# Low-rank adapters of the first token block: by batch in four column quarters, with x at the head of the load queue

## The chip, the cores and the metric

The kernel runs on one core of a Trainium2 chip. Its metric is the device time of one execution in microseconds (us). The engines named here are TensorE (PE; its weight loads are listed apart as PEld), VectorE (DVE), ScalarE (ACT), GpSimd (POOL) and SyncE (SP), which computes nothing and issues most transfers. A queue is the list of transfers that one engine issues, in order.

## The reference

Eight batches of 256 tokens with 1024 features each are the input x. Every batch names one of eight low-rank adapters; its output feeds a gated feed-forward network with FP8 weights and activations, and x is added at the end:

```python
Bx  = einsum('bnr,...->bnr', x, B[adapter_ids])     # rank 16
c   = einsum('bnr,bor->bno', Bx, A[adapter_ids])    # 1024 features
xq  = fp8(clip(c / in_scale))                       # 1024 -> 2752 gate and up
hid = silu(xq @ gate.T * s) * (xq @ up.T * s)
out = x + fp8(hid / in_scale) @ down.T * s          # 2752 -> 1024
```

## The kernel before

Everything is transposed: features lie on the 128 partitions, tokens in the free dimension. The 2048 tokens are four blocks (`NTB`) of 512 (`TB`), two batches of 256 (`SEQ`) in each. The 1024 features are 8 rows (`NH`) of 128, numbered k. The 2752 hidden features are 22 chunks (`NI`), the last one half full.

The program builds its instructions in one pass; an engine takes its own in the order in which they are written, and `multiply` and the copies around it are held to that order. What starts when is then decided by the waits.

**The loads at the start** (lines 394 to 421 of the kernel before). SP issues: the first half of block 0's x (k 0 to 3, 1 MB); a value load of the adapter id of batch 1 and that batch's B (`load_b`, line 366; 68 KB, with the scales of the network in its last columns); x of k 4 to 6; four pieces of A (`load_a_two`, line 373; 16 rows of 2 KB each, two for each batch); x of k 7; the gate and up weights of chunk 0 in two halves and of chunks 1 to 4 whole, 1 MB each (`load_gate_up`, line 391); then block 1's and the other blocks' B, x and A. ScalarE's queue carries the ids and the B of batch 0. GpSimd's queue carries no transfer. A load can start only when the one eight places before it, on the same completion counter, has landed.

**The adapters of a block of two batches** (`two_times_b` and `two_times_a`). TensorE works here with four groups of 32 columns or rows at a time. In B, the four groups are the two batches and two halves of each batch's 256 tokens, so a matmul has 128 columns; for each k four matmuls go to the four groups, into two result tiles `bx`. The 32 stationary columns of a group are 16 of the batch's B and 16 beside them, and A has zeros in the rows of those. Two copies on VectorE and two on ScalarE bring the results into a tile `bm` in which every group's half is beside the other half, so that A can work with all four groups: each row group holds a half of A's output features for one batch. A makes tiles `c` of 2 k rows, VectorE and ScalarE scale them and round them to FP8 (`round_to`, lines 526 and 528) into `xg[t]`.

For block 0 TensorE first does 16 matmuls of zeros (`pass_time`), then B of k 0 to 3, four more matmuls of zeros, B of k 4 to 7, seven of zeros while the copies run, and A.

**Chunk 0** of block 0 is `gate_up(0, 0, turns=(2, 2, 2, 2))`: 16 matmuls of 512 columns, gate and up in turns of two k, so that it can begin when the first rounded rows are there. Chunks 1 to 4 of block 0 follow, then the adapters of block 1 (inside chunk 4), and so on. Blocks 2 and 3 share a pass of four batches (`four_times_b`).

**The output.** For each k of the 8 output rows `times_down` adds up the 22 chunks and `finish` (line 695) multiplies by the scale and adds x. The last k takes its x from a second load into the space of `xg[0]` and `xg[1]`, since it runs in another branch of the program (line 753).

Of the kernel before, what the change touches and what calls it, by code (L numbers as in the profile page):

```python
# [9 lines left out]
F32 = mybir.dt.float32  # L10
# [25 lines left out]

KS = NH // 2

PIECES = ((4, 3, 1), (4, 3, 1), (NH,), (NH,))
FP8_MAX = 448.0  # L40

SAME_MAX = 240.0
# [14 lines left out]
    return ap.bitcast(U16)[..., 0::2]  # L57


def x_of(x4, t, k):  # L60

    first = 0
    for n in PIECES[t]:
        if k < first + n:
            break
        first += n
    at = (t * NH + first) * P * TB
    piece = x4[at : at + n * P * TB].rearrange("(p k n) -> p k n", p=P, k=n)
    return piece, first


def x_row(x4, t, k):
    piece, first = x_of(x4, t, k)
    return piece[:, k - first, :]


def gate_up_of(w_gu, c):
# [15 lines left out]
def general(  # L93
# [71 lines left out]
    def adapt(t, lora, b_sb, a_sb):  # L165
        bx = psum.tile([P, TB], F32, tag="ps", name="g_bx")
        for k in range(NH):
            xk = lora.tile([P, TB], F32, tag="xk", name="g_xk", bufs=2)
            nc.sync.dma_start(out=xk, in_=x_row(x4, t, k))
            nc.tensor.matmul(  # L170
                bx, lhsT=b_sb[:, k, :], rhs=xk, start=(k == 0), stop=(k == NH - 1)
            )
        bm = lora.tile([P, TB], F32, tag="bm", name="g_bm")
        for j in range(TB // SEQ):
            b = t * (TB // SEQ) + j
            nc.vector.tensor_scalar(
                bm[:, bass.ts(j, SEQ)],
                bx[:, bass.ts(j, SEQ)],
                mask[:, b : b + 1],
                None,  # L180
                ALU.mult,
            )
        for k in range(NH):
            c = psum.tile([P, TB], F32, tag="ps", name="g_c")
            nc.tensor.matmul(
                c, lhsT=a_sb[:, bass.ts(k, P)], rhs=bm, start=True, stop=True
            )
            for to, s in ((xg, GATE_IN), (xu, UP_IN)):
                v = work.tile([P, TB], F32, tag="v", name="g_v")
                nc.scalar.activation(v, c, AF.Copy, scale=inv[:, s : s + 1])  # L190
                quantize(to[:, k, :], v, P)
# [38 lines left out]
    def down(t, hid):  # L230
        for k in range(NH):
# [25 lines left out]
                    stop=(i == len(tail) - 1),  # L257
                )
            xr = work.tile([P, TB], F32, tag="g", name="g_xr")
            nc.sync.dma_start(out=xr, in_=x_row(x4, t, k))  # L260
            o = work.tile([P, TB], F32, tag="v", name="g_o")
            nc.vector.scalar_tensor_tensor(
                o, in0=y, scalar=down_s, in1=xr, op0=ALU.mult, op1=ALU.add
# [20 lines left out]
def adaln_ffn(  # L284
# [52 lines left out]
    with ExitStack() as fast:  # L337
# [2 lines left out]
        work = fast.enter_context(tc.tile_pool(name="work", bufs=3))  # L340


        xs = [acts.tile([P, NH, TB], F32, name=f"x{t}") for t in range(NTB)]
        xg += [acts.tile([P, NH, TB], FP8, name=f"xg{t}") for t in range(2, NTB)]


# [2 lines left out]

        b_two = [lora.tile([P, 2 * BROW + R], F32, name=f"b{t}") for t in range(2)]
        a_two = [lora.tile([P, H // 2], F32, name=f"a{t}") for t in range(2)]

        b_four = lora.tile([P, 4 * BROW + R], F32, name="b_four")
        a_four = lora.tile([P, H], F32, name="a_four")
        nc.gpsimd.memset(a_two[0], 0.0)
        nc.vector.memset(a_two[1], 0.0)
        for b, n in ((b_two[0], 2), (b_two[1], 2), (b_four, 4)):
            nc.vector.memset(b[:, n * BROW :], 0.0)  # L360

# [5 lines left out]
                out=b[:, i * BROW : (i + 1) * BROW], in_=b8[bass.ds(adapter * P, P), :]  # L367
            )

        def load_a_two(t, j, adapter):  # L370
            for g in range(2):
                row = 32 * (2 * g + j) + R * j
                nc.sync.dma_start(
                    out=a_two[t][row : row + R],
                    in_=a8[bass.ds(adapter * 2 * R + g * R, R), :],
                )

        def load_x(t, k):
            piece, first = x_of(x4, t, k)
            ks = slice(first, first + piece.shape[1])  # L380
            nc.sync.dma_start(out=xs[t][:, ks, :], in_=piece)

        w_of = {}

# [6 lines left out]
                nc.sync.dma_start(out=w[:, bass.ts(i, n)], in_=src[:, bass.ts(i, n)])  # L391
            w_of[c] = w

        load_x(0, 0)
        load_b(b_two[0], 0, adapter_of(0, nc.scalar), nc.scalar)
        second = adapter_of(1, nc.sync)
        load_b(b_two[0], 1, second, nc.sync)


        load_x(0, 4)  # L400
        load_a_two(0, 1, second)
        load_a_two(0, 0, adapter_of(0, nc.sync))
        load_x(0, 7)
        for c in range(NFIRST):
            load_gate_up(c, parts=1 if c else 2)
        adapters = [adapter_of(2 + q, nc.sync) for q in range(6)]
        for j in range(2):
            load_b(b_two[1], j, adapters[j], nc.sync)
        for k in (0, 4, 7):
            load_x(1, k)  # L410
        for j in range(2):
            load_a_two(1, j, adapters.pop(0))

        for t in (2, 3):
            load_x(t, 0)
# [64 lines left out]
                    stop=(i == n - 1),  # L480
                )

        def times_b(bx, b, n, quads, between=None):


            for k in range(NH):
                for q, (i, row, t, cols) in enumerate(quads):
                    at = i * BROW + k * R - row
                    multiply(
                        bx[q][32 * q : 32 * (q + 1)],  # L490
                        lhsT=b[:, at : at + 32],
                        rhs=xs[t][:, k, cols],
                        start=(k == 0),
                        stop=(k == NH - 1),
                    )
                if between:
                    between(k)

        def two_times_b(t, between=None):


            n = SEQ // 2
            quads = [
                (j, R * j, t, slice(at, at + n))
                for half in range(2)
                for j in range(2)
                for at in (j * SEQ + half * n,)
            ]
            bx = [psum.tile([P, n], F32, tag="ps", name=f"bx{half}") for half in range(2)]
            times_b([bx[q // 2] for q in range(4)], b_two[t], n, quads, between)  # L510
            bm = lora.tile([P, 2, n], F32, tag="bm2", name="bm2", bufs=2)
            for other in range(2):
                for half, copy in enumerate((nc.vector.tensor_copy, nc.scalar.copy)):
                    to = half ^ other
                    tc.keep_in_program_order(
                        copy(  # L516
                            bm[64 * to : 64 * (to + 1), other],
                            bx[half][64 * half : 64 * (half + 1)],
                        )
                    )  # L520
            return bm

        def round_to(to, c, engine):
# [3 lines left out]
            else:  # L527
                nc.scalar.activation(to, c, AF.Copy, scale=scale, saturate=False)  # L528

        def two_times_a(t, bm):  # L530


            n = SEQ // 2
            for part in range(2):
                cs = [psum.tile([P, 2, SEQ], F32, tag="ps", name=f"c{q}") for q in range(4)]
                for other, i in product(range(2), range(2)):
                    for q in range(4):
                        rows = slice(32 * q, 32 * (q + 1))
                        multiply(
                            cs[q][:, i, bass.ts(q // 2 ^ other, n)],  # L540
                            lhsT=a_two[t][rows, bass.ts(2 * part + i, P)],
                            rhs=bm[rows, other],
                            start=True,
                            stop=True,
                        )
                for q in range(4):
                    k = KS * part + 2 * (q // 2)
                    to = xg[t][:, k : k + 2, bass.ts(q % 2, SEQ)]
                    round_to(to, cs[q], nc.vector if q % 2 else nc.scalar)

        def four_times_b():
            quads = [(q, 0, 2 + q // 2, bass.ts(q % 2, SEQ)) for q in range(4)]
            bx = psum.tile([P, SEQ], F32, tag="ps", name="bx")
            times_b([bx] * 4, b_four, SEQ, quads)
            bm = lora.tile([P, SEQ], F32, tag="bm", name="bm", bufs=2)
# [76 lines left out]

        warm = psum.tile([P, TB], F32, tag="ps", name="warm")
        pass_time(warm, 16, TB)
        bm = two_times_b(0, lambda k: pass_time(warm, 4) if k == 3 else None)
        pass_time(warm, 7)
        two_times_a(0, bm)
        gate_up(0, 0, turns=(2, 2, 2, 2))
        for c in range(1, NFIRST - 1):
            gate_up(c, 0)  # L640
# [49 lines left out]

        def finish(k, t, cols, y, x):
            o = outs.tile([P, TB], F32, tag="o", name="o")[:, cols]
            at = slice(t * TB + cols.start, t * TB + cols.stop)
            tc.keep_in_program_order(
                nc.vector.scalar_tensor_tensor(  # L695
                    o, in0=y, scalar=down_s, in1=x, op0=ALU.mult, op1=ALU.add
                )
            )
            tc.keep_in_program_order(nc.sync.dma_start(out=outT[bass.ts(k, P), at], in_=o))
# [30 lines left out]
        for k in range(NH - 1):  # L730
# [9 lines left out]
            if last:  # L740
                ws_last = load_down(k + 1)
                x_last = []

                blocks = x4.rearrange("(t n) -> t n", t=NTB)
                srcs = (
                    blocks[:2, bass.ts(k + 1, P * TB)].rearrange("t (p n) -> p t n", p=P),
                    blocks[2:].rearrange("t (p k n) -> p t k n", p=P, n=TB)[:, :, k + 1, :],
                )
                for i in range(2):
                    x = xg[i].rearrange("p k n -> p (k n)").bitcast(F32)  # L750
                    x = x.rearrange("p (t n) -> p t n", n=TB)
                    x_last += [x[:, j, :] for j in range(2)]
                    nc.sync.dma_start(out=x, in_=srcs[i])
            first = k % 2 == 0
            if first:
                tiles = down_tiles(NTB)
# [128 lines left out]
```

## Time and profile before

| what | us |
|---|---|
| median of 3 runs | 476.14 |
| lowest, highest | 475.85, 476.36 |
| the profiled execution, its own time | 477.12 |
| its span | 475.3 |
| PE busy | 469.8 |
| DVE busy | 105.6 |
| ACT busy | 192.5 |
| POOL busy | 1.0 |

The span runs from the first to the last instruction of the profiled execution; 1.8 us of its time lie around it. Busy time of an engine is the union of its instructions' spans; matmuls overlap, so a busy PE is not one at its peak. In a row of the timeline stand the start and the length in us, the engine, the source line, the operation and its tiles, the number of instructions merged, and in brackets how long the engine had been idle and who released it. In the windows, a transfer share of 1.00 means that all 16 transfer engines were busy.

### The profile page before, as it was taken

What the parts mean: (1) busy time and instruction counts of PE and PEld (TensorE: products, weight loads), DVE (VectorE), ACT (ScalarE), POOL (GpSimd) and SP (SyncE); (2) the same over time, 40 slices, a digit from 0 to 9 for tenths busy, and PEclk for the clock granted to TensorE, in tenths of its full rate; (3) what the DMA queues carried; (4) which work ended last, traced back from release to release, by engine and by line L of the source; (5) the groups of instructions that cost most, each with busy time, mean ns of one, the idle gap of its engine ahead of it and who ended that gap; (6) DMA issues with size and microseconds to landing.
All of it is one profiled execution on the core that took longest, in us unless ns stands there. A gap on an engine that the chain in (4) does not pass through costs nothing.

```text
span 475.3 us, 6009 instructions
## 1 busy us (share of the span) xinstructions
PE 469.8 (99%) x2514; PEld 217.0 (46%) x2514; DVE 105.6 (22%) x163; ACT 192.5 (40%) x249; POOL 1.0 (0%) x7
## 2 busy tenths in 40 slices
PE   8999999999999999999999999999999999999997
PEld 4454544444444444444444444444444444444444
DVE  1333432121212222121212212132120121031031
ACT  1322447995556654533454554359212022021000
POOL 0000000000000000000000000000000000000000
PEclk9999999999999999999999999999999999999999
DMA  8995013422222112222211111123335255063031
GB/s 291 406 405 186 1 48 133 176 88 90 88 88 89 24 66 89 90 88 88 90 30 60 44 62 56 61 83 123 103 146 161 64 185 161 22 213 114 3 116 66
DMA packets 13780, 53.44 MB, mean 112 GB/s; under 512 B 1650, under 2 KB 2930, under 8 KB 10674
## 3 DMA queue, kind: packets, MB, share of 16 engines
q1 hardware_dynamic: 13600, 52.92, 32.1%
q8 instruction: 21, 0.34, 0.3%
q14 instruction: 13, 0.11, 0.1%
q10 hardware_dynamic: 146, 0.07, 0.0%
HBM read 44.60 MB, written 8.39 MB: 111 GB/s over the span
## 4 chain that ended last, share of the span: by engine, by line
PE 96%; DMA 3%; SPq 0%; issue 0%; DVE 0%
PE y L470 62%; PE yd L470 31%; DMA w_gu<-w_gu 2%; PE c L470 1%; PE bx L470 1%; DMA x<-x 1%; DMA ids_i<-ids 0%; SPq L363 0%; SPq L366 0%; DVE o L695 0%; PE count L470 0%
## 5 line engine op out<-in xcount | busy, mean ns | idle before, releaser
L470 PE MATMUL y<-xg,w_gu 128*128 128x512 fp8e4 x1376 | 298.4, 379 | 0.9 <-DMA w_gu<-w_gu 0.9
L470 PEld LDWEIGHTS <-w_gu 128*128 128x128 bf16 x1376 | 134.0, 98 | 163.8 <-DMA w_gu<-w_gu 1.8
L470 PE MATMUL yd<-hid,w_d 128*128 128x512 fp8e4 (+2 forms) x693 | 146.0, 373 | 0.0
L609 ACT ACTIVATE g<-y,gate_s 128x512 f32<-128x512 f32 (+1 forms) x88 | 59.8, 681 | 137.2 <-PE y L470 137.2
L610 DVE SCALAR_TENSOR_TENSOR hid<-y,up_by_down,g 128x512 fp8e4<-128x512 f32 x84 | 63.1, 751 | 220.3 <-PE y L470 162.2
L470 PEld LDWEIGHTS <-w_d 128*128 128x128 bf16 x693 | 66.6, 98 | 79.0 <-issue 1.7
L456 ACT ACTIVATE junk<-w_d 128x1408 bf16<-128x1408 uint16 (+1 forms) x16 | 21.2, 1324 | 88.4 <-DMA w_d<-w_d 88.3
L695 DVE SCALAR_TENSOR_TENSOR o<-yd,down_s,x 128x512 f32<-128x512 f32 x28 | 20.0, 748 | 107.4 <-PE yd L470 92.8
L456 ACT ACTIVATE junk<-w_gu 128x2048 bf16<-128x2048 uint16 (+1 forms) x22 | 41.0, 1863 | 0.0
L463 ACT ACTIVATE junk<-hid 128x2048 bf16<-128x2048 fp8e4 x21 | 40.0, 1905 | 0.4
L463 ACT ACTIVATE junk<-xg 128x2048 bf16<-128x2048 fp8e4 x8 | 15.3, 1909 | 0.3
L528 ACT ACTIVATE xg<-c,inv 128x512 fp8e4<-128x512 f32 x16 | 9.7, 688 | 8.6 <-PE c L470 8.6
L526 DVE TENSOR_SCALAR xg<-c,inv 128x512 fp8e4<-128x512 f32 x16 | 10.9, 744 | 2.8 <-PE c L470 2.8
L470 PE MATMUL warm<-zeros 128*128 128x512 bf16 (+1 forms) x27 | 6.5, 402 | 1.2 <-DVE zeros L309 1.2
L695 DVE SCALAR_TENSOR_TENSOR o<-yd,down_s,xg 128x512 f32<-128x512 f32 (+2 forms) x5 | 3.2, 644 | 12.3 <-PE yd L470 12.3
L516 ACT COPY bm<-bx 64x128 f32<-64x128 f32 x4 | 1.0, 262 | 9.7 <-PE bx L470 9.6
L470 PE MATMUL bx<-x,b 128*32 128x128 f32 x128 | 4.3, 276 | 0.6 <-DMA x<-x 0.6
L470 PEld LDWEIGHTS <-zeros 128*128 128x128 bf16 x27 | 2.6, 116 | 4.7 <-issue 3.0
L470 PE MATMUL c<-bm,a 32*128 32x128 f32 x128 | 4.3, 277 | 0.0
L456 ACT ACTIVATION_READ_ACCUMULATOR junk<-w_gu 128x1 f32 x22 | 4.2, 191 | 0.0
L470 PEld LDWEIGHTS c<-bm,a 32*128 32x128 f32 x128 | 3.9, 186 | 0.5 <-ACT bm L516 0.4
L470 PE MATMUL yd<-hid_tail,w_dt 64*128 64x512 bf16 (+1 forms) x32 | 4.1, 377 | 0.0
(47 smaller groups left out, 41.0 us busy)
## 6 DMA issues: line engine op xcount, KB each, us to landing
w_gu<-w_gu SPq DMA_DIRECT2D x20, 1024.0 KB, 4.8
outT<-o SPq DMA_DIRECT2D x31, 256.0 KB, 2.2
w_d<-w_d SPq DMA_DIRECT2D x8, 704.0 KB, 4.8
w_d<-w_d SPq DMA_DIRECT2D x8, 640.0 KB, 3.9
x<-x SPq DMA_DIRECT2D x2, 2048.0 KB, 11.1
x<-x SPq DMA_DIRECT2D x2, 1024.0 KB, 8.6
x<-x SPq DMA_DIRECT2D x2, 768.0 KB, 9.5
w_gu<-w_gu SPq DMA_DIRECT2D x3, 512.0 KB, 3.8
```

Of the source, the lines that this page charges most:

```text
L456: nc.scalar.activation(junk_like(w), low(w), AF.Copy, accum_out=lows[:rows, column : column + 1])
L463: nc.scalar.activation(junk_like(q), q, AF.Square, accum_out=squares[:rows, column : column + 1])
L470: tc.keep_in_program_order(nc.tensor.matmul(*args, **kwargs))
L516: copy(bm[64 * to : 64 * (to + 1), other], bx[half][64 * half : 64 * (half + 1)],)
L526: nc.vector.tensor_scalar(to, c, scale, None, ALU.mult, saturate=False)
L528: nc.scalar.activation(to, c, AF.Copy, scale=scale, saturate=False)
L609: nc.scalar.activation(g[rows], gates, AF.Silu, scale=gate_s[: gates.shape[0]])
L610: nc.vector.scalar_tensor_tensor(to, in0=ups, scalar=up_by_down[rows], in1=g[rows], op0=ALU.mult, op1=ALU.mult, saturate=False,)
L695: nc.vector.scalar_tensor_tensor(o, in0=y, scalar=down_s, in1=x, op0=ALU.mult, op1=ALU.add)
```

## The change

Block 0's adapters are done batch by batch. `one_times_b(j)` gives each of the four groups a quarter of one batch's 256 tokens, so a matmul has 64 columns, and its stationary columns are that batch's for all four. `one_times_a(j, bm)` has the two quarters beside each other and makes 128 columns a matmul. Each row group needs its own 16 rows of A, so a batch's A is loaded four times (two halves of A, each twice), into a tile of its own. The order on TensorE becomes: 16 matmuls of zeros, B of batch 0, seven of zeros, A of batch 0, B of batch 1, seven of zeros, A of batch 1, chunk 0. The roundings are 256 columns instead of 512, and twice as many. Block 1 keeps its pass.

In memory, block 0's x is laid out by batch, and in pieces: batch 0 with k 0 to 3 and k 4 to 7, batch 1 with k 0 to 6 and k 7. SP issues these four first and the weights of chunks 0 to 4 right behind them. ScalarE's queue loads both batches' B, each after a value load of its id; GpSimd's queue loads both batches' A, each batch's four pieces after a value load. What comes after the weights on SP is as before. The second load of x for the last k becomes five loads instead of two, and `finish` reads block 0's x as two runs of 256.

```diff
-PIECES = ((4, 3, 1), (4, 3, 1), (NH,), (NH,))
+PIECES = (
+    ((0, SEQ, 0, 4), (0, SEQ, 4, 4), (SEQ, SEQ, 0, 7), (SEQ, SEQ, 7, 1)),
+    ((0, TB, 0, 4), (0, TB, 4, 3), (0, TB, 7, 1)),
+    ((0, TB, 0, NH),),
+    ((0, TB, 0, NH),),
+)
...
-        xs = [acts.tile([P, NH, TB], F32, name=f"x{t}") for t in range(NTB)]
+        x_first = acts.tile([P, 2, NH, SEQ], F32, name="x0")
+        xs = [x_first.rearrange("p j k n -> p k j n")]
+        xs += [acts.tile([P, NH, TB], F32, name=f"x{t}") for t in range(1, NTB)]
...
-        a_two = [lora.tile([P, H // 2], F32, name=f"a{t}") for t in range(2)]
+        a_one = [lora.tile([P, H // 2], F32, name=f"a0{j}") for j in range(2)]
+        a_two = lora.tile([P, H // 2], F32, name="a1")
...
-        load_x(0, 0)
-        load_b(b_two[0], 0, adapter_of(0, nc.scalar), nc.scalar)
-        second = adapter_of(1, nc.sync)
-        load_b(b_two[0], 1, second, nc.sync)
-        load_x(0, 4)
-        load_a_two(0, 1, second)
-        load_a_two(0, 0, adapter_of(0, nc.sync))
-        load_x(0, 7)
+        for i in range(len(PIECES[0])):
+            load_x(0, i)
+        for j in range(2):
+            load_b(b_two[0], j, adapter_of(j, nc.scalar), nc.scalar)
+            adapter = adapter_of(j, nc.gpsimd)
+            for q in range(4):
+                load_a_half(a_one[j], q, q // 2, j, adapter, nc.gpsimd)
         for c in range(NFIRST):
             load_gate_up(c, parts=1 if c else 2)
...
+        def one_times_b(j):
+            n = SEQ // 4
+            x = x_first[:, j]
+            quads = [
+                (j, R * j, x[:, :, at : at + n])
+                for half in range(2)
+                for at in (half * n, (2 + half) * n)
+            ]
+            bx = [psum.tile([P, n], F32, tag="ps", name=f"bx{half}") for half in range(2)]
+            times_b([bx[q // 2] for q in range(4)], b_two[0], n, quads)
+            bm = lora.tile([P, 2, n], F32, tag="bm1", name="bm1", bufs=2)
+            for other in range(2):
+                for half, copy in enumerate((nc.vector.tensor_copy, nc.scalar.copy)):
+                    to = half ^ other
+                    tc.keep_in_program_order(
+                        copy(
+                            bm[64 * to : 64 * (to + 1), half],
+                            bx[half][64 * half : 64 * (half + 1)],
+                        )
+                    )
+            return bm
...
+        def one_times_a(j, bm):
+            n = SEQ // 2
+            for part in range(2):
+                cs = [psum.tile([P, 2, n], F32, tag="ps", name=f"c{q}") for q in range(4)]
+                for i, q in product(range(2), range(4)):
+                    rows = slice(32 * q, 32 * (q + 1))
+                    multiply(
+                        cs[q][:, i],
+                        lhsT=a_one[j][rows, bass.ts(2 * part + i, P)],
+                        rhs=bm[rows].rearrange("p a n -> p (a n)"),
+                        start=True,
+                        stop=True,
+                    )
+                for g, half in product(range(2), range(2)):
+                    k = KS * part + 2 * g
+                    at = j * SEQ + half * n
+                    round_to(
+                        xg[0][:, k : k + 2, at : at + n],
+                        cs[2 * g + half],
+                        nc.vector if half else nc.scalar,
+                    )
...
         pass_time(warm, 16, TB)
-        bm = two_times_b(0, lambda k: pass_time(warm, 4) if k == 3 else None)
-        pass_time(warm, 7)
-        two_times_a(0, bm)
+        for j in range(2):
+            bm = one_times_b(j)
+            pass_time(psum.tile([P, TB], F32, tag="ps", name="warm"), 7)
+            one_times_a(j, bm)
         gate_up(0, 0, turns=(2, 2, 2, 2))
...
-                    nc.sync.dma_start(out=x, in_=srcs[i])
+                    for t in (2 * i, 2 * i + 1):
+                        for at, src in x_rows(x4, t, k + 1):
+                            nc.sync.dma_start(out=x_last[t][:, at], in_=src)
```

## The prediction

> **What bounds the kernel now.** I read the page's totals and its chain of waits first, then the chain in order of time, then the timeline of the first 17 us, then the same stretch cut into windows.
>
> ```profile
> span 475.3 us, 6009 instructions
> PE   469.8 (99%) x2514; PEld 217.0 (46%) x2514; DVE 105.6 (22%) x163; ACT 192.5 (40%) x249; POOL 1.0 (0%) x7
> PE y L470 62%; PE yd L470 31%; DMA w_gu<-w_gu 2%; PE c L470 1%; PE bx L470 1%; DMA x<-x 1%; DMA ids_i<-ids 0%; SPq L363 0%; SPq L366 0%; DVE o L695 0%; PE count L470 0%
> ```
>
> TensorE is the bound, so only its idle time and the start of its steady work can move. The chain in order of time (start, length, what) says where that start is:
>
> ```profile
> 3.33 4.97 DMA x<-x
> 8.30 0.02 issue
> 8.32 8.85 DMA w_gu<-w_gu
> 17.17 0.05 issue
> 17.21 13.12 PE y L470 x60
> 30.34 1.88 PE bx L470 x64
> ...
> 58.69 264.29 PE y L470 x1224
> 322.98 121.08 PE yd L470 x570
> ```
>
> From 17.21 us TensorE works without a stop to 472.5; 60 matmuls in 13.12 us are 0.219 each. Before it the chain is transfers: the second weight tile (chunk 1) lands at 17.17. A change to the first 17 us moves the end one for one, by what it does to the start of chunk 1 (call it S, now 17.2). The timeline there:
>
> ```profile
> 6.71 1.08 PE L470 MATMUL bx<-x,b 128*32 128x128 f32 x32
> 9.59 0.43 PE L470 MATMUL bx<-x,b 128*32 128x128 f32 x8 [0.38 <-DMA x<-x]
> 10.05 0.60 DVE L516 COPY bm<-bx 64x128 f32<-64x128 f32 x2 [3.46 <-PE bx L470]
> 10.45 2.17 PE L470 MATMUL c<-bm,a 32*128 32x128 f32 x64
> 11.68 2.73 DVE L526 TENSOR_SCALAR xg<-c,inv 128x512 fp8e4<-128x512 f32 x4 [1.03 <-PE c L470]
> 12.58 1.89 PE L470 MATMUL y<-xg,w_gu 128*128 128x512 fp8e4 x8
> 14.70 1.90 PE L470 MATMUL y<-xg,w_gu 128*128 128x512 fp8e4 x8 [0.23 <-DMA w_gu<-w_gu]
> ```
>
> The adapters finish at 12.58, chunk 0 needs 16 x 0.219 = 3.5 us and could end at 16.1; it waits for the second half of its weights and then chunk 1 waits to 17.2. So the adapters have about 1.1 us to spare, and the transfers have none. How full the transfers are (length, busy of PE, PEld, DVE, ACT, POOL, clock, DMA share, GB/s):
>
> ```profile
> 3.00:7.50 4.50, 4.50 (x42) 2.06 (x43) 0.51 (x6) 0.00 (x0) 0.00 (x0) 1.00 1.01 406
> 7.50:8.50 1.00, 0.78 (x24) 0.41 (x20) 0.00 (x0) 0.00 (x0) 0.00 (x0) 1.00 0.70 168
> 11.50:17.20 5.70, 4.86 (x55) 2.34 (x49) 3.00 (x5) 3.11 (x5) 0.00 (x0) 1.00 0.99 387
> ```
>
> They are full but for one hole, 7.5 to 8.5 us, where the four A loads pass and the last x and the weights were issued late (6.62 and 7.09 us).
>
> **What the Trainium skill says.** DMA: Bandwidth & Descriptors, section on issuing engines, says that DMAs of all issuers share the 16 engines and a second issuer saves issue time only. The trace agrees: the b issued by ScalarE landed 3.2 us after its issue, that by SP 3.3. Its sections Specifications and Anatomy of one DMA price a GpSimd (software) DMA at about 1 us to the first byte and 2.0 us + bytes/436 GB/s in all; no GpSimd DMA is in this trace. TensorE: Matmul & The Clock Gate, section "Wait — 56ns, not 53.3ns?", gives a floor of about 25 ns between starts of small matmuls; the trace's nearest row is 30 ns (64 records in 1.88 us at 128 columns). The same page, section "What's actually happening", says that an idle window of about 3.4 us halves the clock; the trace, whose longest gap is under 1 us, shows 1.0 throughout.
>
> **The change part by part.**
>
> *Issue order.* SP now issues four x pieces and the weights from 0.75 us on, some 0.42 us each, with no value load, b or A in between; the first weights go out at about 2.4 us, not 7.09. Since the engines are full from 3.0 us, this only closes the hole. Idle engine time there is about 5 us of 16 engines (from the packet records, 11 of 16 busy for 1 us), so it gives back 0.3 us of every later landing. SP then reaches its six value loads some 4.7 us earlier, and what follows (b, x and A of block 1) is bound by bandwidth anyway: it lands up to 31 us in a stream that stays full to 41.
>
> *More bytes.* A of block 0 goes from four 32 KB loads to eight, a quarter for each row group. A packet of 2 KB took 84 ns by the packet records, plus 59 in the mean for contention (16 rows lie on few ports): 4 more x 0.143 = 0.57 us on every engine. Smaller x rows (4 KB took 159 ns against 154 for half of an 8 KB one; 1 KB rows) add about 0.1. Sum: -0.3 + 0.57 + 0.1 = +0.36. Chunk 1 then lands at 17.17 + 0.36 = 17.5. Ends: the landing records show that 11 of the 16 engines had their part of chunk 1 by 15.0, and the slowest lags 2.4 us behind the median 14.8. Without that lag it is 15.1; with a further 1 us of it from the new queue, 18.5. I take 17.5, because nothing in the edit touches what the lagging engines did between 10 and 14.6 us.
>
> *Adapters on TensorE.* Before: one pass over both batches, split by k as x lands. After: batch 0 whole, batch 1 whole. The first matmul still starts at 6.71, behind the 16 passes of zeros. One B of a batch has 64 records of 64 columns: 64 x 25 ns = 1.6 us by the skill's floor (0.95 if half of the 1.88 row, 1.88 if columns save nothing). Four copies 0.55 (10.05 to 10.65 above; shorter tiles may save 0.1): A starts at 8.86. A of a batch is half of the 2.17 row, 1.08: to 9.95. Batch 1 takes over the first result buffers, so it waits for their rounding: 8.86 + 0.54 + 0.12 + 0.49 = 10.0. The 0.49 is a 128x256 rounding on VectorE, between the 0.351 (128 columns) and 0.750 (512) of the final multiply-adds; 0.12 is the hand-over seen from 11.52 to 11.64. B of batch 1 ends at 11.6 (its x lands near 9.3, not binding), copies 12.15, half of A 12.7, first rounding 13.3. So chunk 0 starts at 13.3, 0.7 later than now, and ends at 16.8. Ends: with the low B price 15.5, with the high one 17.4. The other roundings, eight per engine where there were four, come at 0.49 for each 0.87 of matmuls: hidden.
>
> *GpSimd's queue.* It holds 1.0 us of work before; now two value loads and eight A loads, one after the other. The first can go at about 2.9 (ScalarE's first after the same wait went at 2.88), the second value load takes about 0.6. With d per load, and 2.08 - 1.0 = 1.1 from its end to landing (the skill's prices), the last A lands at 2.9 + 0.6 + 8d + 1.1 = 4.6 + 8d, and S from it is 0.54 + 0.12 + 0.49 + 3.5 = 4.65 later: 9.25 + 8d. I take d = 1.0 (the first-byte price): A at 12.6, S = 17.25, just under the 17.5. Ends: d = 0.42 (SP's row with its registers) gives 12.6, hidden; d = 2.08, nothing overlapped, gives 25.9. What waits behind a late A is all of TensorE's stream.
>
> *ScalarE's queue.* Two b loads, at 2.9 and some 0.9 later; the second lands near 7.3 and is needed by the last k of batch 0, at about 8.1. Hidden with 0.8 to spare.
>
> *The end.* Five loads for the last x instead of two: three more at 0.4 us on SP, which after 317.83 + 2.10 waits till 323.04 for TensorE: hidden. The final multiply-add reads block 0's x in two runs; VectorE is idle 107 us before that group: hidden.
>
> *Sum.* S = max(16.8, 17.5, 17.25) = 17.5, against 17.2: +0.3 us. The profiled execution would go from 477.12 to 477.4 (span 475.3 to 475.6, 1.8 around it). The median of the runs is 476.14, 1.0 below the profiled one; the same step gives 476.5.
>
> **The rivals.**
>
> *A comes late.* The one mechanism that ends on the slow side: the second batch's A in GpSimd's queue. It decides from d = 1.03 us, and passes 0.2% (0.95 us, about what a measurement of this kernel can tell from no change) at d = 1.11. At d = 1.3 S is 19.65: +2.5 us, 478.6. For it: eight loads in series, each through software. Against it: 16 rows a load are few descriptors. If TensorE then also idles past a clock window, about 3.4 us run at half speed, 1.7 us more: near 480.3.
>
> *The lag goes and the small matmuls are cheap.* Chunk 1 lands at 15.1, and TensorE, at 0.95 us a B, is ready at 15.5: S = 15.5, -1.7 us, 474.4. For it: most engines deliver by 15. Against it: it needs both, and d under 0.78.
>
> *The lag goes alone.* TensorE bounds at 16.8: -0.4 us, 475.7, which is inside the likeliest case's range.
>
> **How the numbers follow.** Start bound by transfers or by TensorE within 0.2% of now: 0.50 (476.5, own range 475.6 to 477.1). A late: 0.36 (477.1 to 479.4), A late with the clock down: 0.06. Start clearly earlier: 0.08. So faster 0.08, same 0.50, slower 0.42. The range leaves out most of the early case and the far end of the late one: 475.3 to 479.4.
>
> **What would show it.** Right: chunk 1's first matmul waits for w_gu at about 17.5; no hole of transfers at 7.5 to 8.5; chunk 0 starts near 13.3; each B pass of a batch takes 1.6 us. Wrong: a wait of c for A's load with TensorE idle before the second batch's c (GpSimd late); chunk 1 running straight on from chunk 0 (the lag gone); a clock below 1.0 in the first slices; or TensorE waiting at block 1's bx near 30 us, which I cost at nothing.

## The result, and the profile after

| | before | after |
|---|---|---|
| median | 476.25 | 484.24 |
| lowest, highest | 475.85, 477.19 | 483.03, 484.74 |
| the profiled execution | 477.12 | 484.74 |
| its span | 475.3 | 483.1 |
| TensorE's first matmul of block 1's adapters | 30.34 | 38.02 |

The changed kernel takes 1.0161 of the time before (95% interval 1.0137 to 1.0185), 8.0 us more, where the prediction had 476.5 and at most 479.4. The last row is the shortest way to the place: of the span's 7.8 us, 7.7 are there before block 1 begins, and from there to the end both kernels take 445 us. So all of it arises in the first 25 us, where the prediction looked for the effect, but it is 7.7 us where 0.3 was forecast.

The page's span, clock row and chain of waits of the changed kernel:

```profile
span 483.1 us, 6191 instructions
...
PEclk8899999999999999999999999999999999999999
...
PE y L484 62%; PE yd L484 31%; PE c L484 2%; DMA b<-b 2%; PE bx L484 1%; PE warm L484 0%; ACT L313 0%; ACTq L375 0%; ACTq L378 0%; ACTq L312 0%; ACT xg L564 0%; DVE o L759 0%; PE count L484 0%
```

The weights and x, which stood in the chain before, are gone from it; B has come in. The two 8s in the clock row are new as well: in the first 24 us TensorE lost full speed twice. The chain in order of time (start, length, what) shows the new path:

```profile
4.16 7.46 DMA b<-b
...
11.65 0.44 PE bx L484 x8
...
17.20 2.13 issue
...
19.82 18.20 PE y L484 x76
38.02 1.89 PE bx L484 x64
```

Three things are to be seen. The load of batch 1's B, issued by ScalarE at 4.16, takes 7.46 us to land, and the last eight matmuls of batch 0's B wait for it, since the 32 stationary columns of its last k reach into the columns of batch 1. Then a gap of 2.13 us stands inside A of batch 1 with nothing that the profile can name ("issue"). And 76 matmuls of `y` take 18.20 us, where 16.5 is their time at full clock (0.216 to 0.219 us each in the steady stretches of both kernels). TensorE's own timeline (start, length, engine, line, operation, in brackets idle time and releaser):

```profile
9.87 2.22 PE L484 MATMUL bx<-x,b 128*32 128x64 f32 x64 [2.55 <-DMA b<-b]
...
14.20 1.14 PE L484 MATMUL bx<-x,b 128*32 128x64 f32 x64
...
19.33 0.49 PE L484 MATMUL c<-bm,a 32*128 32x128 f32 x3 [2.13 <-issue]
```

The first B matmul starts at 9.87, not 6.71: its B landed at 9.74, 6.7 us after its issue. Before, the same instruction on the same queue took 3.2. And the windows of this stretch (length, busy of PE, PEld, DVE, ACT, POOL, clock, share of the transfer engines, GB/s):

```profile
7.50:8.50 1.00, 0.00 (x0) 0.00 (x0) 0.00 (x0) 0.00 (x0) 0.80 (x2) 1.00 1.02 352
8.50:11.50 3.00, 1.63 (x56) 1.51 (x56) 0.51 (x6) 0.00 (x0) 0.48 (x1) 0.68 1.03 310
11.50:15.00 3.50, 3.33 (x105) 2.68 (x105) 1.72 (x6) 1.75 (x6) 0.00 (x0) 0.79 1.05 301
15.00:17.20 2.20, 2.17 (x60) 1.71 (x50) 1.14 (x4) 1.07 (x5) 0.00 (x0) 1.00 1.03 417
...
19.80:23.30 3.50, 3.50 (x10) 1.28 (x10) 0.48 (x1) 0.41 (x1) 0.00 (x0) 0.51 1.02 414
```

The hole of the transfers at 7.5 to 8.5 is closed (1.02, it was 0.70), and TensorE idles through it. The transfer engines count as full from 8.5 to 15.0, but move only 301 to 310 GB/s; before, the full stretches that the prediction shows moved 387 to 406. GpSimd's queue has loads under way then. That its queue is the cause is not shown: e11 (below), with no load on it, moved 248 GB/s at a share of 1.06 from 8.5 to 10.0, while the same small loads of A went through ScalarE's queue. The last row is the second stretch of half clock, at the start of `y`. Chunk 1's weights land at 16.92, 0.25 earlier than before, and nothing waits for them any more.

**Where the 7.7 us are.** The `y` stream of 76 matmuls can be dated back from block 1: before, 30.34 - 16.5 = 13.8; after, it began at 19.82 and lost 18.20 - 16.5 = 1.7 to the clock. So 6.0 us are a later start and 1.7 the clock. Of the 6.0, 2.1 are the gap and the other 3.9 the late B with what it made slow. The experiments take these apart.

### The profile page after: what moved, and what is told of

Read it like the earlier page. It is cut to its first block, busy times and chain, and to the rows that moved or that the text cites. A ratio compares the mean times of both kernels' runs of the same rounds, so it can differ in the third digit from the quotient of the medians.

```text
span 483.1 us, 6191 instructions
## 1 busy us (share of the span) xinstructions
PE 473.9 (98%) x2581; PEld 219.7 (45%) x2581; DVE 107.1 (22%) x170; ACT 193.6 (40%) x255; POOL 5.0 (1%) x15
## 4 chain that ended last, share of the span: by engine, by line
PE 96%; DMA 2%; issue 1%; ACTq 0%; ACT 0%; DVE 0%
PE y L484 62%; PE yd L484 31%; PE c L484 2%; DMA b<-b 2%; PE bx L484 1%; PE warm L484 0%; ACT L313 0%; ACTq L375 0%; ACTq L378 0%; ACTq L312 0%; ACT xg L564 0%; DVE o L759 0%; PE count L484 0%
## 5 line engine op out<-in xcount | busy, mean ns | idle before, releaser
L564 ACT ACTIVATE xg<-c,inv 128x512 fp8e4<-128x512 f32 (+1 forms) x20 | 10.5, 602 | 11.4 <-PE c L484 11.4
L562 DVE TENSOR_SCALAR xg<-c,inv 128x512 fp8e4<-128x512 f32 (+1 forms) x20 | 11.6, 637 | 5.6 <-PE c L484 5.6
L484 PE MATMUL warm<-zeros 128*128 128x512 bf16 (+1 forms) x30 | 7.5, 422 | 1.3 <-DVE zeros L315 1.3
L484 PE MATMUL bx<-x,b 128*32 128x64 f32 (+1 forms) x192 | 5.3, 269 | 2.7 <-DMA b<-b 2.5
L484 PEld LDWEIGHTS bx<-x,b 128*32 128x32 f32 x192 | 4.4, 129 | 4.0 <-issue 3.0
```

The source lines that it names most:

```text
L484: tc.keep_in_program_order(nc.tensor.matmul(*args, **kwargs))
L562: nc.vector.tensor_scalar(to, c, scale, None, ALU.mult, saturate=False)
```

## The experiments

Two theories. *The order*: x and the weights stand ahead of B and A, so B lands with what was issued before it; lost clock and gap follow. *The split*: the adapters by batch have more steps in a row, and these cost the time. A third was A on GpSimd's queue alone, the rival of the prediction. All times are medians; the kernel before, run beside them, had 476.6 to 476.8. The last column is read from the one profiled execution of each; it was 12.58 before and 19.75 in the changed kernel.

| run | kernel | median | ratio to before (95%) | chunk 0 starts |
|---|---|---|---|---|
| e1 | before, new issue order and queues only | 482.30 | 1.0119 (1.0096 to 1.0142) | 17.82 |
| e2 | changed, B early | 481.85 | 1.0116 (1.0084 to 1.0148) | 18.62 |
| e3 | changed, no seven zeros | 482.92 | 1.0138 (1.0109 to 1.0167) | 18.30 |
| e4 | changed, more zeros first | 484.33 | 1.0168 (1.0139 to 1.0196) | 20.51 |
| e5 | changed, B early, A on ScalarE and SyncE | 478.64 | 1.0035 (1.0023 to 1.0047) | 16.04 |
| e6 | e5 with two long zeros for seven | 478.48 | 1.0036 (1.0023 to 1.0050) | 15.86 |
| e7 | before, A on GpSimd's queue only | 477.93 | 1.0028 (1.0020 to 1.0035) | 15.29 |
| e8 | before, A on ScalarE's queue only | 476.21 | 0.9993 (0.9984 to 1.0003) | 12.66 |
| e9 | changed, two long zeros for seven | 483.55 | 1.0131 (1.0112 to 1.0149) | 19.36 |
| e11 | changed, B early, A on ScalarE, two long zeros | 480.97 | 1.0098 (1.0078 to 1.0119) | 15.52 |

**The new order without the split (e1).** The adapters stay as before.

```diff
...
-        load_x(0, 0)
-        load_b(b_two[0], 0, adapter_of(0, nc.scalar), nc.scalar)
-        second = adapter_of(1, nc.sync)
-        load_b(b_two[0], 1, second, nc.sync)
-        load_x(0, 4)
-        load_a_two(0, 1, second)
-        load_a_two(0, 0, adapter_of(0, nc.sync))
-        load_x(0, 7)
+        for k in (0, 4, 7):
+            load_x(0, k)
+        for j in range(2):
+            load_b(b_two[0], j, adapter_of(j, nc.scalar), nc.scalar)
+            load_a_two(0, j, adapter_of(j, nc.gpsimd), nc.gpsimd)
```

> The kernel before with the new issue order alone: x of block 0 first on SP, the weights right behind, both B on ScalarE's queue, A (still four loads) on GpSimd's; the adapters stay one pass over both batches. If B waits behind the x that SP has issued before it: B of batch 0 lands near 9.8 and of batch 1 near 11.6 (after: 9.75 and 11.61, before 6.06 and 6.25), the first matmul of B starts near 11.6 instead of 6.7, and the clock falls to half once; start of chunk 1 near 21.3, time near 480. If the batch-by-batch work is what costs: within 1 us of before (476.3).

482.30: the order and the queues alone cost 5.5 us, without the split. TensorE's timeline of this run:

```profile
8.91 0.38 PE L465 MATMUL bx<-x,b 128*32 128x128 f32 x2 [1.85 <-DMA b<-b]
11.34 1.08 PE L465 MATMUL bx<-x,b 128*32 128x128 f32 x30 [2.06 <-DMA b<-b]
...
17.82 6.42 PE L465 MATMUL y<-xg,w_gu 128*128 128x512 fp8e4 x29
```

The two B landed at 8.77 and 11.30 (6.06 and 6.25 before). Chunk 1's weights landed at 15.02, 2.2 earlier than before: the order does what it looks made for, but TensorE, which begins chunk 0 only at 17.82, cannot use it.

**The changed kernel with B early (e2).** Batch 0's B stays on ScalarE's queue, issued at 3.00; what differs for it is only that SyncE has issued 1 MB of x by then and not 2.

```diff
-        for i in range(len(PIECES[0])):
+        for i in range(2):
+            load_x(0, i)
+        for j, queue in enumerate((nc.scalar, nc.sync)):
+            load_b(b_two[0], j, adapter_of(j, queue), queue)
+        for i in range(2, 4):
             load_x(0, i)
         for j in range(2):
-            load_b(b_two[0], j, adapter_of(j, nc.scalar), nc.scalar)
```

> The changed kernel with B placed as before: two pieces of x, then SP's value load and B of batch 1, then batch 1's x and the weights; B of batch 0 alone on ScalarE; A stays on GpSimd. If B alone was late: B lands by 6.3, the first matmul starts at 6.9, no half clock at 9.6, time near 480. If A on GpSimd is as late as B (its last piece landed at 15.65 in the changed kernel, 0.2 us before its first reader): c of batch 1 still starts near 15.7, time 483 to 484.

B landed at 6.27, 3.3 us after its issue. That settles the first cause: not ScalarE's queue, but what another queue put in front. The time came down only to 481.85, for the next operand is late too:

```profile
7.51 1.10 PE L487 MATMUL bx<-x,b 128*32 128x64 f32 x64
...
15.99 0.94 PE L487 MATMUL c<-bm,a 32*128 32x128 f32 x23 [0.43 <-DMA a<-a]
18.20 0.49 PE L487 MATMUL c<-bm,a 32*128 32x128 f32 x3 [1.26 <-issue]
```

A's last load lands at 15.85, and the nameless gap is there again, three matmuls before the end of `c`, as in the changed kernel.

**The zeros and the gap (e3, e4, e9).** Three edits that change nothing but the matmuls of zeros:

```diff
 e3:
-            pass_time(psum.tile([P, TB], F32, tag="ps", name="warm"), 7)
 e4:
-        pass_time(warm, 16, TB)
+        pass_time(warm, 28, TB)
 e9:
-            pass_time(psum.tile([P, TB], F32, tag="ps", name="warm"), 7)
+            pass_time(psum.tile([P, TB], F32, tag="ps", name="warm"), 2, TB)
```

> The changed kernel without the seven matmuls of zeros after each B: 28 TensorE instructions fewer. If the gap of 2.1 us inside c of batch 1 is a wait for TensorE's next block of instructions, at a fixed count of them: the crossing moves 28 records later in the work, into chunk 0, where queued matmuls of 512 columns cover it; the gap and the half clock after it (19.8 to 23.2) go, time 480.4 (3.8 less). If the gap belongs to a wait of c for data, or the zeros are needed for the clock: 484 or more, gap in the same place.

> The changed kernel with 28 matmuls of zeros at the start instead of 16, so that TensorE is busy until B lands: 24 instructions more. If the first half clock (9.6 to 13.0) costs what it slows: B of batch 0 still waits for the second B at 11.6, so 0.3 to 0.5 us less, 483.8; the gap of 2.1 us comes 24 records earlier in the work, near the middle of c. If the clock is the main cost: 1.7 us less, 482.5.

> The changed kernel, but each time seven zero matmuls of 128 columns follow a B, two of 512 stand in their place: TensorE is kept busy as long and has 20 fewer records before chunk 0 (two passes each less). If the 2.1 us gap at the 449th record is a wait for the next block of instructions, counted in instructions, the gap moves behind the end of A of batch 1, into chunk 0, or goes, and with it the second half clock: steady work starts some 1 to 2 us earlier and the median is near 481 (480.0 to 482.5). If the gap belongs to the adapters' own waits (the results of B, the roundings), it stays where it is and the median stays at 484 (483.3 to 485). The first half clock (9.6 to 13.0) comes from the late B and stays in both.

Without the zeros (e3) the gap is gone, but the clock is at half from 14.02 to 20.84, through two windows of 3.41 us, and the median is only 1.3 us below the changed kernel's. With twelve more zeros first (e4) TensorE idles 1.11 and 1.34 us for the two B, and in the execution shown the clock stays whole; yet the gap comes 12 matmuls sooner and is no shorter:

```profile
16.58 1.03 PE L484 MATMUL c<-bm,a 32*128 32x128 f32 x17
19.86 0.72 PE L484 MATMUL c<-bm,a 32*128 32x128 f32 x15 [2.24 <-issue]
```

After 17 of 32 matmuls of `c` instead of 29: twelve more before it, twelve fewer to go. The gap stands at a count of TensorE's instructions, not at a tile. In the changed kernel, e2, e4 and e11 (below) it comes after the same 449 records of matmuls and weight loads, at 17.2, 16.9, 17.6 and 17.0 us, in `c` in three of them and in `y` in the fourth. In all four it ends 2.56 to 2.59 us after the first packet of a transfer that the packet records call "instruction" (a queue of its own, blocks of 16 KB; starts at 16.74, 15.63, 17.27 and 14.92). The Trainium skill, Runtime: NRT & Kernel Launch, section "Instruction fetch mechanics", says that an engine's instructions are fetched in blocks of 16 KiB (256 instructions) while it executes, with the cost of a boundary "mostly hidden". The block size agrees with these packets; hidden it was not, 2.1 us in the changed kernel. In e9, with ten matmuls fewer, the packet starts at 17.34, so the block would be there at 19.9; the 449th record begins at 20.44, and there is no gap. In the seven other profiled executions, the one of before among them, the 449th record comes 1.3 to 11.2 us after that moment, and none has the gap. So the reading as a wait for the next block fits all twelve; what sets the time of the fetch, which differs by 2.4 us among the four with a gap, was not found.

e9 got rid of the gap and its median is still only 0.7 us lower, short of its expectation. Its windows (columns as above):

```profile
9.70:13.10 3.40, 2.34 (x65) 1.85 (x66) 0.64 (x7) 0.08 (x1) 0.00 (x0) 0.50 1.03 306
13.10:16.50 3.40, 3.40 (x60) 2.45 (x62) 1.67 (x6) 1.74 (x6) 0.00 (x0) 0.50 1.04 361
```

TensorE waits 2.55 and 0.84 us for the two B and the clock is at half for two windows in a row. The median hides something here: in the execution shown, the computing ends at 478.44, 2.1 us sooner than in the changed kernel (480.52), but from there to the end of the span it takes 3.86 us and not 2.56. With four executions each, the intervals of e3 and e9 overlap with that of the changed kernel (1.0137 to 1.0185), so neither gain is clear of the noise. As long as B is late, most of the loss stays in all three: without the gap (e3, e9) there are still two windows of half clock, and without the half clock (e4) there is still the gap.

**B early and A on hardware queues (e5, e6).** The changed kernel with B early; A of batch 0 on ScalarE's queue and of batch 1 on SyncE's; the last x and the weights behind.

```diff
-        for i in range(len(PIECES[0])):
+        for i in range(2):
             load_x(0, i)
-        for j in range(2):
-            load_b(b_two[0], j, adapter_of(j, nc.scalar), nc.scalar)
-            adapter = adapter_of(j, nc.gpsimd)
+        queues = (nc.scalar, nc.sync)
+        ids_of = [adapter_of(j, queue) for j, queue in enumerate(queues)]
+        for j, queue in enumerate(queues):
+            load_b(b_two[0], j, ids_of[j], queue)
+        load_x(0, 2)
+        for j, queue in enumerate(queues):
             for q in range(4):
-                load_a_half(a_one[j], q, q // 2, j, adapter, nc.gpsimd)
+                load_a_half(a_one[j], q, q // 2, j, ids_of[j], queue)
+        load_x(0, 3)
```

> The batch-by-batch work of the changed kernel with B and A early: B of batch 0 on ScalarE, of batch 1 on SP, behind half of batch 0's x only; then batch 1's first x on SP, A of batch 0 on ScalarE's queue and A of batch 1 on SP's, then the last x and the weights; nothing on GpSimd. If late B and A are what costs: first matmul of B near 6.9, c of batch 1 near 11.6; then the next block of TensorE's instructions still falls inside c of batch 1 (record 449), gap of up to 2.5 us, time 477.3 to 479. If batch-by-batch work itself costs: 480 or more. If the instruction block is nothing: 476.

> The same with two matmuls of zeros of 512 columns in place of seven of 128 after each B: as long, 20 TensorE instructions fewer. If the instruction block causes the gap: it falls into chunk 0 and is covered; no gap, time 475.4 to 476.7, 1.5 to 2.5 less than the run with seven. Otherwise as that run.

478.64: with the split kept, 6.0 of the 8 us are back. From TensorE's timeline of e5:

```profile
6.68 1.10 PE L488 MATMUL bx<-x,b 128*32 128x64 f32 x64 [0.44 <-DMA b<-b]
10.08 1.96 PE L488 MATMUL c<-bm,a 32*128 32x128 f32 x30 [1.24 <-DMA a<-a]
11.98 1.94 PE L488 MATMUL bx<-x,b 128*32 128x64 f32 x64
```

From SyncE's:

```profile
10.46 3.63 SPq L404 DMA_DIRECT2D w_gu<-w_gu  x6
```

The first B pass starts where the prediction had it (6.71). What is left on TensorE is A of batch 0, whose second load landed at 10.04 with `c` waiting since 8.85, and half a clock from 10.93 to 14.34, in which B of batch 1 takes 1.94 us instead of 1.10. (This execution took 479.37; three at full clock took 477.98 to 478.78.) The weights are late as well: SyncE, with A of batch 1 ahead of them, issued them from 10.46 on (7.09 before), and chunk 1's landed at 18.54. Even with no wait and a full clock chunk 1 could not have begun sooner, 1.3 us after the 17.21 of before. e6, with two long zeros, gives the same time, against its expectation of a gain: there is no gap in e5 to take away, since the block's packet came at 11.64, far ahead of its use.

**A's queue alone, in the kernel before (e7, e8).** In e7 the four loads of A go to GpSimd's queue, in e8 to ScalarE's behind batch 0's B, batch 0's first; nothing else is changed. The diff of e8:

```diff
...
         load_x(0, 4)
-        load_a_two(0, 1, second)
-        load_a_two(0, 0, adapter_of(0, nc.sync))
+        load_a_two(0, 0, first, nc.scalar)
+        load_a_two(0, 1, adapter_of(1, nc.scalar), nc.scalar)
         load_x(0, 7)
```

> The kernel before with A of block 0 alone moved to GpSimd's queue (four loads); SP then issues x and the weights without it. If GpSimd's loads are late whatever else is done: the last A lands near 12.5 instead of 9.0, c starts near 12.5 instead of 10.4, chunk 1 near 18.2, time 477.3. If A is only late behind more x: c on time, and the weights come earlier than before, 475.5.

> The kernel before with A of block 0 alone moved to ScalarE's queue, behind the B of batch 0; SP then issues x and the weights without it. If what is issued early on a hardware queue is served early: A lands by 10.4, c on time, chunk 1's weights land near 15.5 instead of 17.2, time 475.2 (1 us less). If A queues behind the weights: A after 12, time 477 or more.

TensorE's timeline of e7, then of e8:

```profile
11.37 3.98 PE L470 MATMUL c<-bm,a 32*128 32x128 f32 x64 [0.87 <-DMA a<-a]
15.29 9.02 PE L470 MATMUL y<-xg,w_gu 128*128 128x512 fp8e4 x41
```

```profile
10.53 2.17 PE L471 MATMUL c<-bm,a 32*128 32x128 f32 x64
12.66 11.60 PE L471 MATMUL y<-xg,w_gu 128*128 128x512 fp8e4 x53
```

On GpSimd's queue A lands at 8.60, 9.12, 11.24 and 11.71, each 4.9 to 5.8 us after its issue; before, on SyncE's, it was there by 9.00. In the execution shown, which took 479.33, `c` waits till 11.37 and then runs at half clock, 3.98 us instead of 2.17. Most others kept the clock and took 477.7 to 478.1: so A's lateness alone is 1.3 us, and the half clock comes on top. On ScalarE's queue it lands by 9.43, and `y` runs unbroken from 12.66, over chunk 1's weights, which land at 15.84. That is the best version seen: 476.21, but with an interval of 0.9984 to 1.0003 it isn't told apart from the kernel before.

**The change mended in one place more (e11).** e2 with all eight A on ScalarE's queue and two long zeros for seven.

```diff
 on e2:
-            adapter = adapter_of(j, nc.gpsimd)
+            adapter = adapter_of(1, nc.scalar) if j else first
...
-                load_a_half(a_one[j], q, q // 2, j, adapter, nc.gpsimd)
+                load_a_half(a_one[j], q, q // 2, j, adapter, nc.scalar)
...
-            pass_time(psum.tile([P, TB], F32, tag="ps", name="warm"), 7)
+            pass_time(psum.tile([P, TB], F32, tag="ps", name="warm"), 2, TB)
```

> The changed kernel with its batch-by-batch adapters, but both B ahead of the bulk (batch 0's on ScalarE's queue, batch 1's on SyncE's behind batch 0's x), all eight A on ScalarE's hardware queue behind batch 0's B, two zero matmuls of 512 columns in place of seven of 128, and the weights still right behind x. If the loss is that B and A come late, and what follows from it (clock, gap), and not the splitting of the adapters by batch, then B lands by 6.5, A by 11, the clock stays whole or loses at most one window, and the median is within 1.5 us of the kernel before: 475.5 to 478.2. If the split itself costs (more passes, two chains of copies and roundings), it stays at 479 or above with all operands there.

480.97, outside the 475.5 to 478.2 that the order's theory gave. The timeline says what it had overlooked:

```profile
6.21 4.09 ACTq L384 DMA_DIRECT2D a<-a  x4
...
10.34 0.43 ACT L532 COPY bm<-bx 64x64 f32<-64x64 f32 x2 [7.75 <-DMA a<-a]
10.87 1.29 PE L488 MATMUL c<-bm,a 32*128 32x128 f32 x32 [2.08 <-ACT bm L532]
```

ScalarE stands at its issues of batch 1's A: the third and the fourth go out at 9.42 and 9.94, right after loads ahead of them, batch 0's second and third piece of A, have landed at 9.40 and 9.83, and the last issue ends at 10.30. Its two copies of B's result come next in its order and run from 10.34, and TensorE waits 2.1 us for them. VectorE's two copies of the same result ran from 8.29. ScalarE's lateness is not all of it: the last A of batch 0 landed at 10.03, so with punctual copies `c` would have gained less than 1 us of the 2.1 (an estimate from these times), and the last A of batch 1 landed at 14.18, after its `c` had begun at 13.79, against the 11 that was expected. The gap after 449 records follows (0.51, in `y`). This execution kept its full clock; the other five, which took 479.67 to 483.10, had a mean clock of 0.993 to 0.996. So B was early at last, but A was still late, and a late issuer stood beside it. e11 says nothing for the split's own price: these waits are the queue's.

**What these leave of the two theories.** The order and the queues without the split cost 5.5 us (e1). GpSimd's queue without the order costs 1.3 (e7); in e1 its last A, at 12.54, is hidden behind the late B, since `c` starts only at 15.55. With B early and A on hardware queues, the kernel with the split is 1.8 to 2.0 us slower than before (e5, e6). That is no price of the split alone: e5's profile has a wait for A, a window of half clock and weights that land 1.4 us later than before, and e11's weights, at 18.35, are late too. Whether a split with all operands in place would cost nothing was not shown by any run.

## Why the prediction was wrong

**The step that failed** is "ScalarE's queue": two b loads, the second landing "near 7.3", "Hidden with 0.8 to spare". It took the landing time of before, 3.2 us, and carried it over to a queue order in which twice as much x was issued ahead. The loads landed at 9.74 and 11.61. The number was in the profile already: before, x's first 1 MB landed at 5.74 and B at 6.06, right behind it, so the 3.2 us were the rest of that megabyte and no property of the load. After, B (issued at 3.02) lands between x's third and fourth pieces (9.03 and 10.12), again with what was issued just ahead. The prediction even stated that all issuers share the engines, and used it for the weights alone. Its step on the issue order, "this only closes the hole", is the same error from the other end: the new order issued 2 MB of x ahead of B where 1 MB had stood, and that moved B as well as the weights.

**The adapters on TensorE.** B of batch 0 was to end at 8.3 and ended at 12.09, 3.8 later. From there the steps' lengths were nearly right: to A's start 0.79 us (0.55 taken); from it to batch 1's B 1.3 (1.14 taken). B of batch 1 took 1.14 at full clock where 1.6 was taken: 17.8 ns a record, under the floor of 25 that I priced with, and near the low end of 0.95. Without the gap `c` would have ended near 17.7, and chunk 0 begun there instead of at 13.3: +4.4.

**Not in the sum at all:** the gap of 2.1 us. I read "issue" in the chain as nothing. By the count it comes from the longer list: the batch-by-batch pass puts 67 matmuls and as many weight loads more ahead of chunk 0, and so moves the 449th record into the adapters. Before, it is reached at 27.6 us, and the instruction packet has come at 13.89.

**The clock** was in a rival, behind an idle window of about 3.4 us. The Trainium skill, TensorE: Matmul & The Clock Gate, section "What's actually happening", has that window, and the 3.41 us of half clock agree with its length. The idle time that it takes is another matter: a half window followed on 2.55 us in the changed kernel and on 1.24 in e5, while e4 and e11 idled 2.24 and 2.08 at a stretch and kept their clock in the executions shown. The threshold is not known from these runs; the price is 1.7 us for a window full of matmuls.

**A on GpSimd** was the named rival, with the wrong term in charge. Its d, taken as 1.0, is 0.61 from issue to issue, so all eight were issued by 9.04, not 11.5. But 1.1 us from there to the landing was 6.6: the last A landed at 15.65, not 12.6. In the changed kernel this is hidden, by 0.2 us, because B is later still; e2 uncovers it. That small loads through that queue wait among the large ones was open to the same argument as B's.

**Right:** the place (one for one from the start of the stream: 7.7 of 7.8 us); the closed hole of the transfers; the landing of chunk 1's weights, at 16.92 against 17.5, though the prediction had them bind and nothing waited for them; the rest of the program and the end, at 445 us in both; the loads for the last x, hidden. With late operands S, the start of chunk 1, is 38.02 - 60 x 0.218 = 24.9 against the 17.5 of the sum: +3.8 late B, +0.6 longer steps and slow clock behind it, +2.1 gap, +1.7 clock in chunk 0 come to 8.2 over the 16.8 that was TensorE's own term.

## What to carry to other kernels

A landing time read from a profile belongs to the bytes that were issued ahead of it, on the other queues too (e1, e2); when loads are put in another order, take each small operand that starts a chain and ask what now lands before it. Full transfer engines are worth nothing if the first operand comes last: in e1, weights that land 2.2 us sooner did not make up for two small B loads behind the bulk. Where several waits lie over one another, mending one shows little (e3, e4, e9), and moving a load to the queue of an engine that computes puts that engine's next work behind the issue, for as long as the issue has to wait (e11).

## What was not expected of the hardware

- While the eight small loads of A were under way, the 16 transfer engines counted as full but moved 301 to 310 GB/s, and 417 right after. These loads landed about 1 us apart at the end (12.77, 13.97, 14.77, 15.65), 32 KB each. In e11, with the same loads on ScalarE's queue, it was 248 for 1.5 us; the cause is open.
- TensorE stopped for 0.5 to 2.2 us at the same instruction count in four kernels, each time until 2.6 us after an instruction packet.
- A pause of TensorE costs its own length and often, but not always, a window of 3.41 us at half clock after it: 1.24 us of idling were followed by one in e5, and 2.24 were not in e4.
